# Turning the second half's context and x by small loads and VectorE, the last product token by token, in a new order

## The chip, the cores and the metric

The kernel runs on one core of a Trainium2 chip. The metric is the device time of one execution in microseconds. A core has five engines with instruction queues of their own, each taken in order: TensorE (PE in the profile; its weight loads are the row PEld), VectorE (DVE), ScalarE (ACT), GpSimd (POOL) and SyncE (SP), which here issues every transfer between the large memory (HBM) and the on-chip memory (SBUF). TensorE writes into eight banks of a second on-chip memory, PSUM. All data are 32-bit floats.

## The reference

One cross-attention block with a two-layer network behind it, for 8 sequences of 256 tokens, 512 features, 16 heads of 32. The mask is all ones.

```python
x = layer_norm(hidden_states, ln1_w, ln1_b)
q = (x @ q_w + q_b)                      # 16 heads of 32
k = (encoder_hidden_states @ k_w + k_b)
v = (encoder_hidden_states @ v_w + v_b)
attn = softmax(q k^T / sqrt(32))
out = (attn v) @ cproj_w + cproj_b
hidden = out + hidden_states
y = layer_norm(hidden, ln2_w, ln2_b)
y = gelu(y @ fc_w + fc_b, approximate=True)     # 512 -> 2048
return hidden + (y @ proj_w + proj_b)           # 2048 -> 512
```

## The kernel before

The 2048 tokens are worked through in two halves g = 0, 1 of 1024 tokens (four sequences each). In each half the stages are: context and x come in and are turned so that features lie on partitions; q, k and v are projected; sixteen units of attention follow (four heads of one sequence each); then the output projection (o), the second layer norm (y), the wide layer (fc) and the narrow layer (pd). Stages of the two halves overlap.

**Seven products.** A projection is split into 2 x 2 blocks and worked out as seven block products with sums of blocks around them instead of eight (`quad`, `sums`, `operands`). The products of one quad are called P1 to P7; they collect in three PSUM banks X, Y and W, and VectorE, ScalarE or GpSimd add the banks into four result blocks. The two layers of the network do this twice, seven outer products of seven inner ones (`grown2` for fc, `grown` for pd). All products are issued by one helper, `mm` (the profile's L642); a 32-bit matmul is two instructions in the profile. The sums of weights for the network are made once, by VectorE and GpSimd during the first attention, and stored to HBM (fcd, prd) by SyncE.

**Turning.** `turned` (L713) does it on TensorE: four transposes of 128x128 fill one PSUM bank (L729), and a copy, for x with the layer norm's scale and bias, takes it to SBUF. Context and x of both halves go this way, and y of the first half: eight banks each. `moved` (L734) does it without TensorE, and only y of the second half goes this way: eight stores of normalised tiles to HBM (yd), sixteen loads of 128 KB that bring 32x32 blocks into place in pieces of 128 bytes (yb), eight VectorE transposes of 32x32 blocks over 128x512 (L748), and a pass with scale and bias (L752 on ScalarE, L754 on VectorE).

**The narrow layer's end.** `ending` (L1270 on) runs after four of the seven outer products of pd, when a quarter of the result is complete. The result po lies with features on partitions. For three quarters VectorE turns 32x32 blocks (tr, L1311), adds the residual read back from HBM in 128-byte pieces (rq, out), and SyncE stores it in such pieces (so). The last quarter, features 256 to 511 of the first 512 tokens, is finished by the outer product 4, of the blocks z1t4 and z1i and the weights pl14. In the second half it is turned on TensorE (turn_o, L1289, eight transposes), added to the residual rl (ot), and stored as two tiles (st).

**What sets the order.** PROGRAM lists every step in the order of issue, with the engine behind a colon (V is VectorE, A ScalarE, G GpSimd) where there is a choice; PLACES gives each buffer its slot. Both are tables written out in the kernel. A step's instructions stand in their engine's queue in that order. Buffers share slots, and a name in the profile is that of the slot's first user: `ct` or `q` may hold a weight later on.

## Time and profile before

| what | value |
|---|---|
| median of the runs | 675.18 us (3 runs, 672.50 to 675.52) |
| profiled execution, first to last instruction (span) | 671.4 us |
| median less span | 3.8 us |
| mean granted clock of TensorE | 1.000 of full speed |
| busy: TensorE, VectorE, ScalarE, GpSimd | 662.8, 585.3, 347.3, 345.0 us |
| DMA traffic | 140.97 MB in 174064 packets, 71.9% of 16 engines' span |

The profile is one execution; its own time is the span and what lies around it, and only the span is recorded. A row of the table by windows gives a stretch's start and end, its length, the busy time of TensorE, its weight loads, VectorE, ScalarE and GpSimd with instruction counts in brackets, the granted clock, the busy share of the DMA engines and the rate in GB/s. A group of instructions reads: line, engine, operation, output<-inputs, shapes, count, then busy time and mean nanoseconds, then idle time before them. In the view of one tile, the durations are minimum/median/maximum in ns.

### The profile page before, as it was taken

How to read it: one execution, taken by the hardware profiler on the slowest of the kernel's cores; microseconds unless marked ns; L12 is line 12 of the kernel's file. 1: busy time of each engine (PE TensorE's matmuls, PEld its weight loads, DVE VectorE, ACT ScalarE, POOL GpSimd, SP SyncE). 2: the span in 40 equal slices, each digit the busy share in tenths (PEclk: the TensorE clock that was granted, in tenths of full speed). 3: DMA queues.
4: the chain of work that ended last, by engine and by line, in shares of the span. 5: the costliest groups of instructions: out<-in, count | busy, mean ns of one | idle time of the engine just before them, and what ended most of it. 6: DMA issues, size and time to landing. Idle time of an engine off the chain costs nothing.

```text
span 671.4 us, 11531 instructions
## 1 busy us (share of the span) xinstructions
PE 662.8 (99%) x4001; PEld 497.7 (74%) x4001; DVE 585.3 (87%) x974; ACT 347.3 (52%) x711; POOL 345.0 (51%) x322
## 2 busy tenths in 40 slices
...
GB/s 250 330 291 319 318 285 271 226 290 259 258 186 234 214 136 141 212 273 105 142 111 118 205 158 250 179 254 260 240 206 297 122 240 104 266 80 142 169 186 114
DMA packets 174121, 141.69 MB, mean 211 GB/s; under 512 B 83776, under 2 KB 134512, under 8 KB 174064
## 3 DMA queue, kind: packets, MB, share of 16 engines
q1 hardware_dynamic: 174064, 140.97, 71.9%
...
q14 instruction: 25, 0.20, 0.1%
...
## 4 chain that ended last, share of the span: by engine, by line
PE 86%; DVE 8%; DMA 2%; ACT 2%; SPq 1%; issue 1%; POOL 0%; DVEq 0%; ACTq 0%
PE pd_X L642 14%; PE fc_X L642 14%; PE fc_W L642 7%; PE pd_W L642 7%; PE av L642 7%; PE s L642 4%; PE o_X L642 4%; PE pd_Y L642 4%; PE k_X L642 3%; PE fc_Y L642 3%; PE q_X L642 3%; PE v_X L642 3%; PE v_W L642 2%; DVE mx L1005 2%; PE k_W L642 2%; DMA cq<-in_ctx_dram 2%
## 5 line engine op out<-in xcount | busy, mean ns | idle before, releaser
L622 ACT ACTIVATE pr<-s,cols 128x256 f32<-128x256 f32 x256 | 103.8, 484 | 23.3 <-PE s L642 12.6
L1030 POOL TENSOR_TENSOR pr<-pr,mm 128x512 f32<-128x512 f32 x60 | 76.6, 1307 | 20.0 <-DMA mm<-md 17.0
L1005 DVE TRANSPOSE_TENSOR_REDUCE mx<-pr 128x32 f32<-128x1024 f32 x64 | 77.5, 1223 | 3.8 <-ACT pr L622 3.6
L1033 ACT ACTIVATE pr<-pr 128x1024 f32<-128x1024 f32 x64 | 66.2, 1065 | 7.9 <-DVE pr L1025 5.9
L1210 ACT ACTIVATE h<-h,cols 128x256 f32<-128x256 f32 x128 | 56.2, 501 | 12.0 <-DVE h L633 11.8
L633 DVE TENSOR_TENSOR h<-fc_X,h 128x512 f32<-128x512 f32 x80 | 53.1, 679 | 7.6 <-PE fc_X L642 7.2
L1025 DVE TENSOR_TENSOR pr<-pr,mm 128x1024 f32<-128x1024 f32 x34 | 41.2, 1237 | 0.2 <-DMA mm<-md 0.2
L633 DVE TENSOR_TENSOR h<-fc_W,h 128x512 f32<-128x512 f32 x48 | 32.0, 681 | 6.7 <-PE fc_W L642 6.3
L642 PE MATMUL av<-pr,ones 128*32 128x256 f32 x512 | 34.2, 384 | 0.2
L1012 ACT COPY mx<-mx 32x64 f32<-32x64 f32 x96 | 23.1, 243 | 19.1 <-issue 16.0
L808 ACT ACTIVATE xn_y<-hid,rs_y 128x512 f32<-128x512 f32 x7 | 5.5, 817 | 52.1 <-DVE rs_y L800 52.0
L633 POOL TENSOR_TENSOR h<-h,fl 128x512 f32<-128x512 f32 x12 | 15.6, 1311 | 25.2 <-DVE fl L633 24.9
L642 PEld LDWEIGHTS av<-pr,ones 128*32 128x32 f32 x512 | 14.5, 109 | 18.3 <-issue 4.8
L609 ACT COPY fl<-fc_X 128x512 f32<-128x512 f32 x6 | 3.5, 583 | 40.6 <-PE fc_X L642 38.5
L631 POOL TENSOR_TENSOR z0t<-h,h 128x512 f32<-128x512 f32 x10 | 14.7, 1489 | 11.2 <-issue 10.6
L1013 DVE TENSOR_REDUCE mx<-mx 32x32 f32<-32x256 f32 x32 | 18.3, 575 | 1.2 <-ACT mx L1012 1.0
L633 DVE TENSOR_TENSOR h<-fc_Y,h 128x512 f32<-128x512 f32 x24 | 16.1, 677 | 2.6 <-PE fc_Y L642 2.3
L642 PE MATMUL fc_W<-y1i,fl 128*128 128x256 f32 x72 | 18.1, 380 | 0.0
L633 POOL TENSOR_TENSOR tq<-tq,rq 128x512 f32<-128x512 f32 x8 | 10.1, 1273 | 13.5 <-DVE tq L1311 13.5
L642 PE MATMUL pd_W<-z1i,pl 128*128 128x256 f32 x72 | 16.8, 380 | 0.0
L752 ACT ACTIVATE y<-y,cols 128x512 f32<-128x512 f32 x7 | 5.5, 811 | 21.5 <-DVE y L748 21.5
L642 PE MATMUL fc_X<-y1i,fl 128*128 128x256 f32 x64 | 16.5, 381 | 0.0
...
## 6 DMA issues: line engine op xcount, KB each, us to landing
...
```

Of the source, the lines that this page charges most:

```text
L622: lambda e: nc.scalar.activation(to(), of_(), AF.Identity, bias=bias(), scale=1.0))
L631: nc.gpsimd.tensor_tensor(to()[:, ts(k, 512)], in0()[:, ts(k, 512)], in1()[:, ts(k, 512)], op)
L633: E[e].tensor_tensor(to(), in0(), in1(), op)
L642: nc.tensor.matmul(o(), l(), r(), start=first, stop=True, skip_group_check=True)
L752: nc.scalar.activation(at(r, j, 1, 512), at(r, j, 1, 512), AF.Identity, bias=col(cb_ + c), scale=col(cw_ + c))
L1005: T.op(f"mx{u}_{h}", [("DVE", 1.126)], [(pr[h], None)], [(mx, [h])], lambda e, h=h: nc.vector.tensor_reduce(tile_of(mx)[:, 0:64].rearrange ...
L1012: lambda e, a=a: nc.scalar.copy(tile_of(mx)[0:32, 64 + 64 * a : 128 + 64 * a], tile_of(mx)[32 * a : 32 * a + 32, 64:128]))
L1013: T.op(f"fold{u}", [("DVE", 0.38)], [(mx, [2, 3, 4, 5])], [(mx, [6])], lambda e: nc.vector.tensor_reduce(tile_of(mx)[0:32, 320:352], tile_ ...
L1025: nc.vector.tensor_tensor(p_, p_, m_[:, :, None, :].to_broadcast([P, 2, 2, S]), ALU.subtract)
L1030: E[e].tensor_tensor(p_, p_, at(M, j)[:, None, :].to_broadcast([P, 2, S]), ALU.subtract)
L1033: lambda e, h=h: nc.scalar.activation(tile_of(pr[h]), tile_of(pr[h]), AF.Exp), table="exp")
L1210: lambda e, f=f, b=b, c=c: nc.scalar.activation(at(h[f][b], c), at(h[f][b], c), AF.Gelu_apprx_tanh, bias=col(c_fcb + f * 4 + c), scale=1.0 ...
```

## The change

1. Context and x of the second half go by `moved` instead of `turned`. The context is read in 128-byte pieces straight from its input (cb), with no stores ahead and no scaling pass behind; x is stored after its normalisation (xd), loaded (xb), transposed (xT) and scaled.
2. The inner products of the outer product 4 of the second half's pd swap their operands: the activations are the stationary side, and the weights stream past, so tokens lie on partitions. Each inner product is eight matmuls of 128 columns instead of four of 256. Their sums go straight into the tiles that are stored (ot).
3. What those tiles start from is the quarter as it stands without the product 4, with the residual: VectorE turns it and adds rq, SyncE stores it to a scratch tensor (lo, eight stores) and loads it back (rl, four loads). The transposes on TensorE at the end (turn_o) go. The last stores are three, of one whole tile and two halves.
4. PROGRAM and PLACES are written anew throughout; engines of many steps change, mostly from VectorE to GpSimd. The second batch of warm-up matmuls writes a bank of its own.

The new order at two places. First TensorE's queue at its end, where the last products of pd stand (pd14 is the outer product 4, its banks X, Y, W; ps_o the transposes). Before:

```order
L642 MATMUL pd13_Y_5821<-h1_32_5047,pl13_2_5727 128x256 x4
L642 MATMUL pd14_X_5745<-z1i4_1_5735,pl14_4_5700 128x256 x4
L642 MATMUL pd14_W_5841<-z1i4_3_5803,pl15_3_5591 128x256 x4
L642 MATMUL pd14_X_5745<-z1t4_3_5682,pl14_3_5787 128x256 x4
L642 MATMUL pd14_Y_5857<-z1t4_2_5679,pl13_3_5691 128x256 x4
L1289 MATMUL ps_o11_5865<-ident_64,po1_1_5461 128x128 x2
L1289 MATMUL ps_o01_5869<-ident_64,po1_1_5461 128x128 x2
L642 MATMUL pd14_W_5841<-z1i4_4_5833,pl14_4_5700 128x256 x4
L1289 MATMUL ps_o00_5881<-ident_64,po1_0_5380 128x128 x2
L1289 MATMUL ps_o10_5887<-ident_64,po1_0_5380 128x128 x2
```

And now:

```order
L633 MATMUL pd13_X_5661<-h1_33_5137,pl14_2_5473 128x256 x4
L633 MATMUL pd14_X_5771<-pl15_4_5183,z1t4_0_5676 128x128 x8
L633 MATMUL pd12_W_5714<-z1i2_4_5668,fl107_0_4698 128x256 x4
L633 MATMUL pd14_X_5771<-pl12_3_5501,z1i4_2_5719 128x128 x8
L633 MATMUL pd13_W_5740<-z1i3_4_5749,pl02_4_4365 128x256 x4
L633 MATMUL pd14_X_5771<-pl14_5_5622,z1i4_1_5709 128x128 x8
L633 MATMUL pd14_W_5843<-rl0_5758,z1i4_3_5756 128x128 x8
L633 MATMUL pd14_X_5771<-pl12_1_4994,z1t4_3_5702 128x128 x8
L633 MATMUL pd14_W_5843<-pl13_2_5515,z1i4_4_5814 128x128 x8
L633 MATMUL pd14_Y_5877<-pl14_2_5473,z1t4_2_5578 128x128 x8
```

The eight ps_o transposes are gone; seven groups of eight 128-column matmuls, with z blocks as the second name, take the place of the seven groups of four, and nothing of TensorE's stands behind the last of them.

Second, VectorE's queue where the second half's context comes in, beside the first attention's units (mx and pr are a unit's maxima and scores; c1 the context turned, cb1 as loaded, ps_c1 as transposed by TensorE; the other names are slots that hold q and k sums at that time). Before:

```order
L794 TENSOR_SCALAR rs_x1_0_942<-mv_x1_0_761 128x2
L1025 TENSOR_TENSOR pr000_0_710<-pr000_0_710,mm000_864 128x1024
L1025 TENSOR_TENSOR pr000_1_748<-pr000_1_748,mm000_864 128x1024
L609 COPY c1_10_937<-ps_c1_30_956 128x512
L1005 TENSOR_REDUCE mx022_969<-pr022_1_913 128x2x2x8
L633 TENSOR_TENSOR q0_1_21_731<-q0_1_W_917,q0_1_21_731 128x512
L633 TENSOR_TENSOR v0_0_21_417<-v0_0_W_812,v0_0_21_417 128x512
L1013 TENSOR_REDUCE mx002_879<-mx002_879 32x32
```

And now:

```order
L744 STREAM_TRANSPOSE c1_00_895<-cb1_0_725 128x512
L808 TENSOR_SCALAR q0_1_22_882<-kws1_352,mv_x1_1_776,rs_x1_1_837 128x512
L1011 TENSOR_REDUCE mx020_864<-mx020_864 32x32
L744 STREAM_TRANSPOSE c1_00_895<-cb1_1_620 128x512
L624 TENSOR_TENSOR q0_1_22_882<-q0_1_W_885,q0_1_22_882 128x512
L1003 TENSOR_REDUCE mx002_928<-pr002_0_888 128x2x2x8
L744 STREAM_TRANSPOSE c1_01_846<-cb1_0_725 128x512
L1003 TENSOR_REDUCE mx002_928<-pr002_1_898 128x2x2x8
L1007 STREAM_TRANSPOSE mx002_928<-mx002_928 128x64
L624 TENSOR_TENSOR kw01_359<-v0_0_W_933,kw01_359 128x512
L1003 TENSOR_REDUCE mx022_960<-pr022_1_939 128x2x2x8
L1011 TENSOR_REDUCE mx002_928<-mx002_928 32x32
```

Before, VectorE has one copy of the context here, behind TensorE's transposes, and ScalarE has the other seven; now VectorE has eight transposes that wait for loads, and the maxima of the units 002 and 022 stand between and behind them.

The diff, without the two tables:

```diff
@@ PROGRAM @@
-cq0_00_1 cq0_00_0 rows5 vw00 rows3 kw00 rows6 kw10 turn_c0_00 rows4 turn_c0_10 c0_00:V cq0_01_1 c0_10:V cq0_10_1
...
+cq0_00_0 cq0_00_1 vw00 cq0_01_1 fw0_00_1 cq0_01_0 cq0_11_0 cq0_11_1 vw10 fw0_01_1 turn_c0_00 rows1 turn_c0_10 vw11
@@ -500,6 +490,7 @@
 }
+MOVED = {"c": (1,), "x": (1,), "y": (1,)}
 KINDS = ("pppppppppppppppp", "pppppppppppppppp")
@@ -731,21 +722,28 @@
-    def moved(g, tag, tiles, cw_, cb_):
+    def moved(g, tag, tiles, cw_, cb_, of_=None):
         R = [[Buf(f"{tag}{g}_{J}{L}", "Q", 4) for L in range(2)] for J in range(2)]
-        d = dram(f"{tag}d{g}", [1024, D], 8)
-        for i in range(8):
-            b, f = tiles[i]
-            store(f"{tag}d{g}_{i}", d, [i], [(b, None)], lambda i=i: d.t[ts(i, P), :], f, 0.26)
+        if of_ is None:
+            d = dram(f"{tag}d{g}", [1024, D], 8)
+            src = [(d, None)]
+            for i in range(8):
+                b, f = tiles[i]
+                store(f"{tag}d{g}_{i}", d, [i], [(b, None)], lambda i=i: d.t[ts(i, P), :], f, 0.26)
+        else:
+            src = []
+        whole = (lambda: d.t) if of_ is None else (lambda: of_)
         for c in range(4):
...
                 load(f"{tag}b{g}_{c}{a}", q, [a], lambda q=q, a=a: tile_of(q)[32 * a : 32 * a + 32].rearrange("p (t j) -> p t j", j=32),
-                     lambda a=a, c=c: d.t.rearrange("(t i) (b a j) -> b a i t j", i=32, b=4, a=4)[c, a], 0.33, src=[(d, None)], lead=2.0)
+                     lambda a=a, c=c: whole().rearrange("(t i) (b a j) -> b a i t j", i=32, b=4, a=4)[c, a], 0.33, src=src, lead=2.0)
             for L in range(2):
...
                      lambda e, q=q, r=r, j=j, L=L: nc.vector.transpose(at(r, j, 1, 512), at(q, L, 1, 512)))
+                if cw_ is None:
+                    continue
@@ -1144,7 +1142,7 @@
-    def grown(name, n, place, spare, product_of, cost, wide, before=None, bias={}):
+    def grown(name, n, place, spare, product_of, cost, wide, before=None, bias={}, end=None):
@@ -1153,7 +1151,10 @@
                 dst, add = fused[p]
-                quad(f"{name}{p}", product_of(p), cost, dst, add=add, bias=bias.get(p), n=n, wide=wide)
+                wd = wide
+                if p == 4 and end:
+                    dst, add, wd = end
+                quad(f"{name}{p}", product_of(p), cost, dst, add=add, bias=bias.get(p), n=n, wide=wd)
             else:
@@ -1258,14 +1259,26 @@
                 (lk, lv), (rk, rv) = Lw[q], Ri[q]
+                if g == 1 and p == 4:
+                    return [lk, rk], [
+                        (lambda t=t: bank()[:, ts(t, P)], lambda t=t, c=c: rv()[:, c * 256 + t * P : c * 256 + t * P + P], lambda c=c: lv()[:, ts(c, P)],
+                         first and t == 0 and c == 0)
+                        for t in range(2) for c in range(4)
+                    ]
                 return [lk, rk], [
...
-        rq, tq, view, ot = {}, {}, {}, {}
-        rl = [Buf(f"rl{l}", "P") for l in range(2)] if g == 1 else None
+        rq, tq, view = {}, {}, {}
+        two = lambda t: t.rearrange("p (t n) -> p t n", t=2)
+        if g == 1:
+            rl, ot = [Buf(f"rl{l}", "P", 2) for l in range(2)], [Buf(f"ot{l}", "P", 2) for l in range(2)]
+            part_ = dram("lo", [512, 256], 8)
+
+        def at_end(bufs):
+            return {k: ((bufs[e % 2], [e // 2]), lambda b=bufs[e % 2], i=e // 2: two(tile_of(b))[:, :, ts(i, P)]) for e, k in enumerate(IL)}
@@ -1275,26 +1288,14 @@
             if g == 1 and p == 4:
-                two = lambda t: t.rearrange("p (t n) -> p t n", t=2)
-                for l in range(2):
-                    ot[l] = Buf(f"ot{l}", "P", 2)
-                    load(f"rl{l}", rl[l], None, lambda l=l: two(tile_of(rl[l])),
-                         lambda l=l: h_.t[l * S : (l + 1) * S, ts(I, 256)].rearrange("(t p) n -> p t n", p=P), 0.26, src=[(h_, [l])], lead=3.0)
-                for e in (0, 3, 1, 2):
-                    i, l = divmod(e, 2)
-                    ps = Buf(f"ps_o{i}{l}", "C")
-
-                    def turn(_, ps=ps, l=l, c=2 * I + i):
-                        for t in range(2):
-                            nc.tensor.transpose(tile_of(ps)[:, ts(t, P)], at(po[l], c)[:, ts(t, P)], ident.t)
-                    T.op(f"turn_o{i}{l}", [("PE", 0.225)], [(po[l], [2 * I + i]), (ident, None)], [(ps, None)], turn, mode="full")
-                    plus(f"ot{i}{l}", (ot[l], [i]), (ps, None), (rl[l], None), lambda i=i, l=l: two(tile_of(ot[l]))[:, :, ts(i, P)],
-                         lambda ps=ps: two(tile_of(ps)[:, :256]), lambda i=i, l=l: two(tile_of(rl[l]))[:, :, ts(i, P)], 256)
-                for l in (1, 0):
-                    store(f"st{l}", None, None, [(ot[l], None)], lambda l=l: o_[l * S : (l + 1) * S, ts(I, 256)].rearrange("(t p) n -> p t n", p=P),
-                          lambda l=l: two(tile_of(ot[l])), 0.26)
+                for l, i in ((1, None), (0, 0), (0, 1)):
+                    w = slice(0, 256) if i is None else slice(i * P, i * P + P)
+                    store(f"st{l}{'' if i is None else i}", None, None, [(ot[l], None if i is None else [i])],
+                          lambda l=l, w=w: o_[l * S : (l + 1) * S, 256 + w.start : 256 + w.stop].rearrange("(t p) n -> p t n", p=P),
+                          lambda l=l, w=w: two(tile_of(ot[l]))[:, :, w], 0.26 if i is None else 0.13)
                 return
-            part = (1,) if g == 1 and I else (0, 1)
+            rest = g == 1 and I == 1 and L == 1
+            part = (0, 1)
             last = L == (1 if not I or g else 0)
@@ -1306,17 +1307,28 @@
                              0.165 * len(part), src=[(h_, [2 * x + y for x in part for y in range(2)])], lead=3.0)
-                for l in range(2):
-                    b = 2 * L + l
+                for b in range(4) if rest else (2 * L, 2 * L + 1):
                     T.op(f"tr{g}_{c}{b}", [("DVE", 0.34)], [(po[b], [c])], [(tq[c], [b])], lambda e, b=b, c=c: nc.vector.transpose(at(tq[c], b), at(po[b], c)))
-                plus(f"out{g}_{c}{L}", (tq[c], [2 * L, 2 * L + 1]), (tq[c], [2 * L, 2 * L + 1]), (rq[c], None), lambda c=c: at(tq[c], L, 1, 512),
-                     lambda c=c: at(tq[c], L, 1, 512), lambda c=c: at(rq[c], L, 1, 512), 512, pool_too=True)
-                if last:
+                for h in (0, 1) if rest else (L,):
+                    plus(f"out{g}_{c}{h}", (tq[c], [2 * h, 2 * h + 1]), (tq[c], [2 * h, 2 * h + 1]), (rq[c], None), lambda c=c, h=h: at(tq[c], h, 1, 512),
+                         lambda c=c, h=h: at(tq[c], h, 1, 512), lambda c=c, h=h: at(rq[c], h, 1, 512), 512, pool_too=True)
+                if rest:
+                    half = lambda t, a, h: t[32 * a : 32 * a + 32, 512 * h : 512 * h + 512].rearrange("p (t j) -> p t j", j=32)
+                    piece = lambda m, a, r0, c0: m[r0 : r0 + 512, c0 + 32 * a : c0 + 32 * a + 32].rearrange("(t i) j -> i t j", i=32)
+                    for a in range(4):
+                        store(f"lo{i}{a}", part_, [4 * i + a], [(tq[c], [0, 1])], lambda i=i, a=a: piece(part_.t, a, 0, i * P), lambda c=c, a=a: half(tile_of(tq[c]), a, 0), 0.17)
+                    for a in range(4):
+                        store(f"so{g}_{c}{a}", None, None, [(tq[c], [2, 3])], lambda c=c, a=a: piece(o_, a, 512, c * P), lambda c=c, a=a: half(tile_of(tq[c]), a, 1), 0.17)
+                    for l in range(2):
+                        load(f"rl{l}{i}", rl[l], [i], lambda l=l, i=i: two(tile_of(rl[l]))[:, :, ts(i, P)],
+                             lambda l=l, i=i: part_.t[l * S : (l + 1) * S, ts(i, P)].rearrange("(t p) n -> p t n", p=P), 0.13, src=[(part_, [4 * i + a for a in range(4)])], lead=2.0)
+                elif last:
                     for a in range(4):
...
         grown(f"pd{g}", 256, place, spare, product_of, 1.727, lambda t: t[:, :256], ending,
-              {p: {k: (lambda c=c_pb + 2 * I + e // 2: col(c)) for e, k in enumerate(IL)} for p, I in ((2, 0), (3, 0), (7, 1))})
+              {p: {k: (lambda c=c_pb + 2 * I + e // 2: col(c)) for e, k in enumerate(IL)} for p, I in ((2, 0), (3, 0), (7, 1))},
+              (at_end(ot), at_end(rl), lambda t: two(t[:, :256])) if g == 1 else None)
@@ -1328,15 +1340,16 @@
         if g == 0:
-            T.op("small", [("PE", 0.1)], [], [], lambda e: small(WARM2))
-        ct = token_quarters(g, "c", ef) if g == 0 else token_tiles(g, "c", ef)
+            again = Buf("again", "W")
+            T.op("small", [("PE", 0.1)], [], [(again, None)], lambda e: small(WARM2, tile_of(again)))
+        ct = token_quarters(g, "c", ef) if g == 0 else token_tiles(g, "c", ef) if g not in MOVED["c"] else None
         if g == 0:
             biases()
-        C = turned(g, "c", ct if g == 0 else [(b, lambda b=b: tile_of(b)) for b in ct], plain)
+        C = turned(g, "c", ct if g == 0 else [(b, lambda b=b: tile_of(b)) for b in ct], plain) if g not in MOVED["c"] else moved(g, "c", None, None, None, ef[g * 1024 : g * 1024 + 1024, :])
         T.stream(f"x{g}")
...
         xn = layer_norm(g, "x", [(b, None, lambda b=b: tile_of(b)) for b in xt])
-        X = turned(g, "x", xn, scaled(c_ln1w, c_ln1b))
+        X = turned(g, "x", xn, scaled(c_ln1w, c_ln1b)) if g not in MOVED["x"] else moved(g, "x", xn, c_ln1w, c_ln1b)
         T.stream(f"k{g}")
@@ -1392,7 +1405,7 @@
         yn = layer_norm(g, "y", srcs)
-        Y = moved(g, "y", yn, c_ln2w, c_ln2b) if g in (1,) else turned(g, "y", yn, scaled(c_ln2w, c_ln2b))
+        Y = moved(g, "y", yn, c_ln2w, c_ln2b) if g in MOVED["y"] else turned(g, "y", yn, scaled(c_ln2w, c_ln2b))
         for b in range(4):
...
```

676 lines of the change are left out of this document (333 added, 343 removed).

## The prediction

> **What bounds the kernel now.** I read the page's busy table first, then what TensorE waited for.
>
> ```profile
> span 671.4 us, 11531 instructions
> ...
> PE 662.8 (99%) x4001; PEld 497.7 (74%) x4001; DVE 585.3 (87%) x974; ACT 347.3 (52%) x711; POOL 345.0 (51%) x322
> ...
> q1 hardware_dynamic: 174064, 140.97, 71.9%
> ```
>
> ```profile
> engine line waited for: us in total, times, longest us
> PE ps_y L729 <- DVE rs_y L794: 1.2, 1, 1.2
> PE first L654 <- DVE warm L649: 1.0, 1, 1.0
> PE v_X L642 <- DVE kw L609: 0.5, 1, 0.5
> PE fc_W L642 <- DVE h L633: 0.4, 1, 0.4
> ...
> PE fc_Y L642 <- DVE y L767: 0.2, 1, 0.2
> ```
>
> TensorE is busy 99% of the span and its longest wait is 1.2 us. A busy matmul engine can still run slowly, so I looked in the chain of waits, in order of time, at the pace of whole stretches (start, length, what):
>
> ```profile
> 56.47 1.75 PE ps_x L729 x16
> ...
> 93.98 2.18 PE ps_c L729 x20
> ...
> 457.37 5.18 PE pd_W L642 x24
> ```
>
> A 256-column matmul instruction takes 5.18/24 = 0.216 us, a 128-column transpose 1.75/16 = 0.109 us: time goes as columns, with nothing between. So TensorE bounds the kernel from end to end, and what leaves it leaves the time, as long as the others keep feeding it. How near they are to not doing so, by stage:
>
> ```profile
> core 0: us, PE busy (x) PEld busy (x) DVE busy (x) ACT busy (x) POOL busy (x), PEclk, DMA share, GB/s
> 20.00:60.00 40.00, 39.72 (x143) 23.98 (x142) 37.92 (x74) 16.04 (x25) 16.31 (x20) 1.00 0.93 314
> 60.00:100.00 40.00, 40.00 (x226) 23.01 (x225) 36.80 (x61) 27.18 (x65) 13.39 (x16) 1.00 0.91 306
> 100.00:180.00 80.00, 79.44 (x603) 48.33 (x605) 75.70 (x125) 66.89 (x138) 55.06 (x55) 1.00 0.84 260
> 180.00:260.00 80.00, 79.76 (x668) 48.33 (x664) 76.29 (x128) 74.68 (x165) 63.51 (x53) 1.00 0.61 193
> ```
>
> From 20 to 180 us VectorE idles 9.6 us of 160, and the DMA engines have 40 x 0.07 + 40 x 0.09 + 80 x 0.16 = 19.2 us free. The new work falls into just this stretch.
>
> **Context and x leave TensorE.** Each had eight turns of four 128-column transposes: 64 x 0.109 = 6.98 us of TensorE gone, with the waits between them. Eight PSUM copies go for the context, seven of them ScalarE's; x keeps its scaling as a pass of its own, a copy from PSUM against a pass over SBUF, about even. VectorE gets 16 transposes of 128x512:
>
> ```profile
> L596 SPq DMA_DIRECT2D yb<-yd x16: 302/560/1617, 475.0 to 493.0; - x16
> L748 DVE STREAM_TRANSPOSE y<-yb x8: 664/683/702, 489.3 to 503.9; 128x512 f32<-128x512 f32 x8
> ```
>
> That is 16 x 0.683 = 10.9 us. The new order pays for it: counted in the two programs, VectorE has 111 instead of 134 sums of 128x1024 with both inputs in SBUF, and GpSimd 232 instead of 181 of 128x512.
>
> ```profile
> L1030 POOL TENSOR_TENSOR pr<-pr,mm 128x512 f32<-128x512 f32 x60 | 76.6, 1307 | 20.0 <-DMA mm<-md 17.0
> ...
> L1025 DVE TENSOR_TENSOR pr<-pr,mm 128x1024 f32<-128x1024 f32 x34 | 41.2, 1237 | 0.2 <-DMA mm<-md 0.2
> ```
>
> VectorE: 10.9 - 23 x 1.237 = 17.6 us less; GpSimd: 51 x 1.307 = 66.7 us more of its 326 idle. On their own neither is the bound, so I cost them at nothing; the cover is the idle time just named, and the rivals price its loss.
>
> **The loads.** Context: 8 loads of 256 KB become 16 of 128 KB in 128-byte pieces. x: 8 stores of 256 KB and 16 such loads are added to its loads. The 256 KB transfer costs, at 314 GB/s (20 to 60 us), 0.83 us of all engines. For the small pieces, the second y gives the price, five of its loads in a row on SyncE's queue:
>
> ```profile
> 474.98 4.12 SPq L596 DMA_DIRECT2D yb<-yd  x5
> ```
>
> 0.82 us for each 128 KB. Context adds 16 x 0.82 - 8 x 0.83 = 6.5 us, x 16 x 0.82 + 8 x 0.83 = 19.8 us: 26.3 us against 19.2 free, 7.1 too many. The bounds are nothing (fill-in traffic, the weight sums' stores, steps aside; some loads of x now go out in the first 20 us) and 7.1 us. In the fullest stretch before, 0.93, TensorE lost only 0.28 us of 40, so I take 2.0, nearer to nothing. What waits behind a late load is told by VectorE's rows: two transposes of the context stand ahead of the softmax maxima (TENSOR_REDUCE mx) of the units 002 and 022, and VectorE takes its queue in order; each such wait stops scores, then TensorE. On SyncE's queue an xd store that waits for its normalised tile holds the broadcasts (mm) of the next units. Of x the chain is longer by a store and a load; the order answers by normalising its first tiles some 50 us of TensorE work sooner. If that cover fails, the second half's q products wait.
>
> **The last product by tokens.** Its seven products are now 112 instructions of 128 columns instead of 56 of 256, each with its own weight load. By the transposes' pace they take 112 x 0.109 = 12.2 us, against 56 x 0.216 = 12.1: 0.1 us more. The weight loads, min/median/max ns:
>
> ```profile
> L729 PEld LDWEIGHTS ps_x<-ident,xn_x x20: 139/141/146, 47.6 to 177.1; 128*128 128x128 f32 x20
> ```
>
> ```profile
> L642 PEld LDWEIGHTS v_X<-vw,c x32: 186/190/190, 7.7 to 141.2; 128*128 128x128 f32 x32
> ```
>
> A transpose's load of 141 ns hides under 109 ns streams; a product's takes 190. Nothing in this trace pairs a product's 128-column load with a 128-column stream, so the bounds are 0.109 and 0.190 us each, 0 to 9.1 us in all. The nearest row is the warm-up, 64-column loads under 64-column streams:
>
> ```profile
> 5.89 1.85 PE L654 MATMUL first<-warm 128*64 128x64 f32 x28
> 7.67 1.56 PE L642 MATMUL v_X<-vw,c 128*128 128x256 f32 x6
> ```
>
> 28 in 7.67 - 5.89 = 1.78 us, 0.064 each for half the columns: near the stream's pace, so I take 0.1 us. The Trainium skill, "TensorE: Matmul & The Clock Gate", section "Back-to-back issue gap", says that a stream with a weight load for each matmul is paced by both, about 81 ns where the stream alone is 56 at 128 columns. By that rule, as an estimate, 25 ns x 112 = 2.8 us would be added; the transposes' 109 ns speak against it here.
>
> **The end.** Start, length, engine, operation:
>
> ```profile
> 664.44 0.60 PE L1289 MATMUL ps_o<-ident,po 128*128 128x128 f32 x4
> ...
> 664.88 1.89 PE L642 MATMUL pd_W<-z1i,pl 128*128 128x256 f32 x8
> ...
> 666.61 0.38 PE L1289 MATMUL ps_o<-ident,po 128*128 128x128 f32 x2
> 666.81 0.42 DVE L633 TENSOR_TENSOR po<-pd_W,po 128x256 f32<-128x256 f32 x1 [0.97 <-PE pd_W L642]
> 667.15 0.41 DVE L633 TENSOR_TENSOR ot<-ps_o,pl 128x256 f32<-128x256 f32 x1
> 667.29 0.20 PEld L1289 LDWEIGHTS ps_o<-ident,po 128*128 128x128 f32 x2 [0.54 <-DVE po L633]
> ...
> 667.76 0.43 DVE L633 TENSOR_TENSOR ot<-ps_o,pl 128x256 f32<-128x256 f32 x1 [0.20 <-PE ps_o L1289]
> 668.22 0.39 SPq L602 DMA_DIRECT2D out_dram<-ot  x1
> ```
>
> Four transposes stand ahead of the last product: 664.88 - 664.44 = 0.44 us gone. From that product's last slot, 666.61, to the end at 671.4 pass 4.79 us: sum, transpose, sum, store. Without the transpose: 0.20 to the sum, 0.42 for it, 0.03 to the issue, 671.4 - 668.22 = 3.18 for the store, 3.83 in all, 0.96 less. The residual's way by TensorE is replaced by four VectorE transposes, eight small stores and four loads, done before the last outer product ends; they cost nothing while the stores ahead of the last one drain in time.
>
> **The sum.** 671.4 - 6.98 - 0.44 - 0.96 + 0.1 + 2.0 = 665.1 us of span. The median of the runs shown, 675.18, lies 3.8 above the span; so 668.9 us. A measurement can tell about 0.5% (3.4 us) of this kernel from no change.
>
> **Rivals.** *More than the sum.* The new order is free to close the old waits too. TensorE's nine listed waits, five of them shown, come to 4.3 us, 3.3 without the warm-up's; with the loads hidden (no 2.0) the time is 675.2 - 8.3 - 3.3 = 663.6. For: they lie on VectorE, which gets lighter. Against: every new order makes waits of its own.
>
> *The loads give it back.* All 7.1 us reach TensorE: 675.2 - 8.3 + 7.1 = 674.0, no difference. For: the shares of 0.84 to 0.93. Against: no wait of TensorE for a DMA there before.
>
> *The loads turn it round (slower).* The same queue, but 128-byte pieces among full traffic cost more than 0.82. The overload is 7.1 + 32 x (c - 0.82); it passes 8.3 + 3.4 = 11.7, slower by 0.5%, at c = 0.96 us. One issue of the y loads took 1.617 us on the queue. At c = 1.1 it is 16.1 us, 683 in all. Against: the y loads kept 0.82 while the queues were full.
>
> *VectorE and GpSimd shut each other out.* GpSimd's sums are 1274 ns or far longer:
>
> ```profile
> L631 POOL TENSOR_TENSOR c1t<-c,c1t x4: 1274/1716/2266, 101.2 to 119.1; 128x512 f32<-128x512 f32 x4
> ...
> L633 DVE TENSOR_TENSOR c1t<-c,c x1: 1204/1204/1204, 99.9 to 99.9; 128x1024 f32<-128x1024 f32 x1
> ```
>
> 2266 - 1274 = 0.99 us is most of one such VectorE sum. Up to the first output projection GpSimd has 145 of these instead of 120; if each of the 25 costs VectorE 0.99 us, that is 24.7 us, against 9.6 idle from 20 to 180 and 3.7 from 180 to 260: 11.4 us over, 675.2 - 8.3 + 11.4 = 678.3, no difference. The Trainium skill, "SBUF — State Buffer", section "Who interferes with whom", says that a VectorE instruction with two SBUF inputs and a GpSimd one that reads SBUF cannot run at once. By that rule, the trace agrees (2266 against 1274 ns). Against this rival: VectorE's own such sums get fewer by 23.
>
> *The token-major product is paced by its weight loads*, at 0.190 us each: 9.1 us in place of 0.1, so 668.9 + 9.0 = 677.9, no difference; below 2.9 us of it, still faster (671.8). For: the 190 ns. Against: the warm-up's pace.
>
> **How the numbers follow.** The forecast 0.57; more than the sum 0.14; the loads give it back 0.12; the shut-out 0.07; weight-load pace 0.04; slower by late loads 0.06. Faster takes the first two and half of the weight-load case: 0.73; no change 0.21; slower 0.06. The range goes from 662.5 (old waits closed, a little more at the end) to 677.0 (give-back, and most of the shut-out); it leaves out the late loads and little below.
>
> **What would show it.** Right: a span near 665; no ps_c or ps_x of the second half; seven token-major groups of 1.74 us at the end; about 3.8 us after the last product; no VectorE wait for the context's small loads over 2 us. Wrong: token-major groups near 3 us; TensorE waiting between 60 and 180 us behind VectorE, with the DMA share at 1 there; GpSimd's 128x512 sums well over 1.31 us on the mean.

## The result, and the profile after

| | before | after |
|---|---|---|
| median (14 runs each) | 672.88 us | 678.92 us |
| lowest and highest | 672.10, 675.52 | 674.87, 683.51 |
| profiled span | 671.4 us | 677.6 us |

The ratio is 1.0082 (95%: 1.0062 to 1.0101): slower by 0.8%, where 668.9 us against 675.18, 0.9% less, was forecast. An execution's time lies about 1.8 us above its own span (1.75 to 1.91 in after's fourteen), not 3.8: the 3.8 set the median of three executions against the span of another. That made the forecast of the time too high, so its miss of 10.0 us hides 2.5 of the 12.5 us by which the span was missed (677.6 against 665.1). The page of after, in the lines that the prediction began with (busy time, share, instructions; then the DMA queue):

```profile
span 677.6 us, 11590 instructions
...
PE 660.0 (97%) x3985; PEld 495.9 (73%) x3985; DVE 579.9 (86%) x956; ACT 343.6 (51%) x703; POOL 445.6 (66%) x380
...
q1 hardware_dynamic: 216480, 146.21, 76.7%
```

TensorE is busy 2.8 us less in a span that is 6.2 us longer. What it waited for, the longest first:

```profile
engine line waited for: us in total, times, longest us
PE k_X L633 <- DVE kws L624: 2.8, 1, 2.8
PE av L633 <- ACT pr L1031: 1.5, 4, 0.5
PE pd_X L633 <- DVE z0i L624: 1.3, 2, 1.0
PE fc_W L633 <- DVE e L624: 1.1, 1, 1.1
```

There are 17 such rows and 13.0 us, where before had nine and 4.3. One wait is long; the rest are scattered over the kernel, and behind them stand all four other parties. By stage (columns as in the table of before):

```profile
core 0: us, PE busy (x) PEld busy (x) DVE busy (x) ACT busy (x) POOL busy (x), PEclk, DMA share, GB/s
20.00:60.00 40.00, 37.18 (x137) 23.60 (x136) 33.15 (x68) 13.81 (x22) 24.00 (x27) 0.96 1.02 358
60.00:100.00 40.00, 39.88 (x170) 21.46 (x169) 36.99 (x60) 26.23 (x60) 23.23 (x23) 1.00 0.99 269
100.00:180.00 80.00, 78.74 (x626) 46.91 (x625) 73.91 (x129) 64.32 (x134) 70.25 (x62) 1.00 1.00 278
180.00:260.00 80.00, 77.59 (x575) 46.90 (x573) 75.97 (x117) 74.32 (x163) 70.87 (x54) 1.00 0.76 241
```

The DMA engines are full to 180 us, and from 100 us on GpSimd works 141 of 160 us, where it worked 119. The groups that grew or came (count, busy us, mean ns, idle before):

```profile
L1028 POOL TENSOR_TENSOR pr<-pr,mm 128x512 f32<-128x512 f32 x78 | 108.0, 1413 | 13.6 <-DMA mm<-md 7.0 <-PE fc_X L633 5.9 <-issue 0.5
L1023 DVE TENSOR_TENSOR pr<-pr,mm 128x1024 f32<-128x1024 f32 x25 | 32.1, 1294 | 0.8 <-DMA mm<-md 0.8
...
L744 DVE STREAM_TRANSPOSE y<-yb 128x512 f32<-128x512 f32 x8 | 5.5, 697 | 6.2 <-DMA yb<-yd 6.2
L744 DVE STREAM_TRANSPOSE c<-cb 128x512 f32<-128x512 f32 x8 | 5.3, 684 | 0.0
L744 DVE STREAM_TRANSPOSE x<-xb 128x512 f32<-128x512 f32 x8 | 5.2, 672 | 0.0
```

The transposes of context and x cost what was forecast (10.5 us, 10.9 forecast) and wait for no load. But the same softmax subtraction is 8% dearer on GpSimd than in before (1413 against 1307 ns) and 5% on VectorE (1294 against 1237).

The end went nearly as forecast. The timeline (start, length):

```profile
668.26 1.95 PE L633 MATMUL pd_X<-pl,z1t 128*128 128x128 f32 x16
...
670.05 1.95 PE L633 MATMUL pd_W<-pl,z1i 128*128 128x128 f32 x16
...
671.83 1.95 PE L633 MATMUL pd_Y<-pl,z1t 128*128 128x128 f32 x16
...
673.82 0.42 DVE L624 TENSOR_TENSOR pl<-pd_Y,pl 128x256 f32<-128x256 f32 x1 [1.36 <-PE pd_Y L633]
674.27 0.37 SPq L593 DMA_DIRECT2D out_dram<-pl  x1
```

A token-major group starts 1.79 us after the one ahead of it (1.74 forecast). The prediction counted the end from the last product's last slot; that is 671.83 + 1.79 = 673.62 here, and from there to the span's end pass 3.96 us (4.79 before, 3.83 forecast).

**Where the time went.** For each run of like instructions on TensorE I took the time to the next run's start, less its count by the pace of undisturbed stretches (0.109, 0.216, 0.430 us for 128, 256, 512 columns; 0.058 for warm-up; attention 1.80 us for 32 av and 1.08 for 16 scores). What is left is TensorE's lost time, waits and slow clock alike, in us by stage; records missing from a trace count in it, so some tenths mean nothing.

| kernel | 0-40 | 40-120 | 120-260 | 260-480 | 480-600 | 600- | all |
|---|---|---|---|---|---|---|---|
| before | 3.5 | 2.1 | 6.2 | 7.5 | 1.6 | 0.2 | 21.1 |
| after | 10.3 | 2.2 | 11.3 | 5.2 | 5.4 | 1.1 | 35.4 |
| before_48_out | 3.1 | 5.0 | 11.2 | 8.9 | 1.6 | 0.2 | 30.0 |
| before_48_out_less | 3.7 | 3.8 | 8.1 | 6.1 | 1.6 | 0.2 | 23.4 |
| before_72_added | 3.2 | 1.7 | 4.8 | 8.5 | 1.6 | 0.2 | 20.0 |
| after_72_added | 7.0 | 3.6 | 7.3 | 5.9 | 6.1 | 1.1 | 31.1 |
| after_all_relieved | 7.2 | 2.0 | 8.9 | 6.0 | 5.5 | 1.1 | 30.7 |

So TensorE's own work fell by 7.7 us (72 transposes fewer, 7.85, and 0.1 more for the token-major groups), the end by another 0.4 (0.83, less 0.44 for the four transposes that stood in it), and its lost time rose by 14.3: together the 6.2 us of span. The loss came at three places: the first 40 us, the first attention (120 to 260), and the second half's wide layer (480 to 600). Of the 10.3 us in the first 40, some 3 belong to this execution. The trace records its full clock from 10.36 us on, before's from 5.44 (28 warm-up matmuls took from 6.71 to 10.15 us here, from 5.89 to 7.67 in before), and the clock was halved again behind the wait of 2.8 us. The seven other profiles with after's unchanged start lose 6.6 to 7.3 there.

### The profile page after: what moved, and what is told of

The parts are those of the page before. It is cut to its first block, busy times and chain, and to the rows that moved or that the text cites. A ratio compares the mean times of both kernels' runs of the same rounds, so it can differ in the third digit from the quotient of the medians.

```text
span 677.6 us, 11590 instructions
## 1 busy us (share of the span) xinstructions
PE 660.0 (97%) x3985; PEld 495.9 (73%) x3985; DVE 579.9 (86%) x956; ACT 343.6 (51%) x703; POOL 445.6 (66%) x380
## 4 chain that ended last, share of the span: by engine, by line
PE 68%; DVE 11%; DMA 8%; ACT 5%; POOL 3%; issue 2%; SPq 2%; DVEq 0%; POOLq 0%; ACTq 0%
PE fc_X L633 11%; PE pd_X L633 11%; PE av L633 6%; PE pd_W L633 6%; PE fc_W L633 5%; PE q_X L633 3%; PE s L633 3%; PE fc_Y L633 3%; PE v_X L633 3%; PE o_X L633 3%; PE pd_Y L633 2%; ACT pr L613 2%; DMA fw<-in_L_xattn_fc_w_dram 2%; PE k_X L633 2%; SPq L587 2%
## 5 line engine op out<-in xcount | busy, mean ns | idle before, releaser
L1028 POOL TENSOR_TENSOR pr<-pr,mm 128x512 f32<-128x512 f32 x78 | 108.0, 1413 | 13.6 <-DMA mm<-md 7.0
L624 DVE TENSOR_TENSOR h<-fc_X,h 128x512 f32<-128x512 f32 x80 | 53.6, 680 | 14.1 <-PE fc_X L633 12.9
L1023 DVE TENSOR_TENSOR pr<-pr,mm 128x1024 f32<-128x1024 f32 x25 | 32.1, 1294 | 0.8 <-DMA mm<-md 0.8
L622 POOL TENSOR_TENSOR z1i<-z1t,z1i 128x512 f32<-128x512 f32 x8 | 11.8, 1494 | 17.8 <-DVE z1i L624 17.8
L624 POOL TENSOR_TENSOR tq<-tq,rq 128x512 f32<-128x512 f32 x9 | 11.9, 1330 | 12.8 <-DVE h L624 6.0
L622 POOL TENSOR_TENSOR z0t<-h,z0t 128x512 f32<-128x512 f32 x6 | 10.4, 1750 | 14.5 <-DVE z0t L624 14.5
L750 ACT ACTIVATE y<-y,cols 128x512 f32<-128x512 f32 x5 | 4.0, 813 | 30.9 <-DVE y L744 30.9
L633 PE MATMUL fc_X<-y1i,fl 128*128 128x256 f32 x72 | 18.4, 380 | 0.5 <-DVE h L624 0.5
L633 PE MATMUL pd_W<-z0i,pl 128*128 128x256 f32 x80 | 18.8, 380 | 0.0
L633 PE MATMUL pd_X<-z0i,pl 128*128 128x256 f32 x72 | 16.9, 380 | 1.0 <-DVE z0i L624 1.0
L624 POOL TENSOR_TENSOR po<-po,e 128x256 f32<-128x256 f32 x7 | 6.9, 1001 | 15.2 <-DVE e L624 11.1
```

The lines of the kernel that those rows point to most:

```text
L622: nc.gpsimd.tensor_tensor(to()[:, ts(k, 512)], in0()[:, ts(k, 512)], in1()[:, ts(k, 512)], op)
L624: E[e].tensor_tensor(to(), in0(), in1(), op)
L633: nc.tensor.matmul(o(), l(), r(), start=first, stop=True, skip_group_check=True)
L1023: nc.vector.tensor_tensor(p_, p_, m_[:, :, None, :].to_broadcast([P, 2, 2, S]), ALU.subtract)
L1028: E[e].tensor_tensor(p_, p_, at(M, j)[:, None, :].to_broadcast([P, 2, S]), ALU.subtract)
```

## The experiments

Ratios are to before's runs on the same chip, with 95% intervals; after itself was not timed again beside each of them, so a comparison with it takes its 1.0082 as it stands. The theories, in the order in which they were formed: **A**, the new order loses in its first 40 us, and that stays to the end. **B**, the 128-byte loads fill the DMA engines. **C**, VectorE and GpSimd shut each other out. **D**, VectorE paces the first attention as much as TensorE does, so TensorE's time is not worth its time. **E**, TensorE bounds the kernel and after has many small waits. **F**, several engines are at their limit together. **G**, each mended place keeps what it gains.

**The first 40 us (A).** VectorE's and TensorE's timelines of after at the place:

```profile
25.51 1.23 DVE L624 TENSOR_TENSOR fw0s<-fw,fw 128x1024 f32<-128x1024 f32 x1 [3.92 <-DMA fw<-in_L_xattn_fc_w_dram]
26.65 0.68 DVE L624 TENSOR_TENSOR kws<-kws,kw 128x512 f32<-128x512 f32 x1
```

```profile
27.48 3.62 PE L633 MATMUL k_X<-c0t,kws 128*128 128x512 f32 x4 [2.82 <-DVE kws L624]
```

A sum of fc weights, needed far later, stands in VectorE's queue ahead of kws and waits 3.92 us for its load; TensorE waits 2.82 for kws. kws_first turns the two round:

```diff
-fw1_11_0 fw0s1:V k0_1_t1:A xt0_1 qw00 v0_1_P6 xt0_6 kws2:V xt0_4
+fw1_11_0 k0_1_t1:A xt0_1 qw00 v0_1_P6 xt0_6 kws2:V fw0s1:V xt0_4
```

> One step of VectorE moved, nothing else: the k weights' sum kws2 goes ahead of the fc weights' sum fw0s1, for which VectorE waited 3.9 us on a load. Theory A (the new order loses, first of all in its first 40 us): TensorE's 2.8 us wait for kws and the 3.41 us at half clock behind it (1.7 us lost) go, unless the context's late load then stops TensorE in their place; 675 to 677 us against 679 of the changed kernel. Theory B (the 128-byte loads of context and x fill the queue and cost it): no change, 679. Theory C (VectorE and GpSimd shut each other out): no change, 679.

Measured: 1.0106 (1.0084 to 1.0127). The wait is gone, and another has come (where the tables differ, so do the line numbers):

```profile
23.53 1.88 PE L622 MATMUL k_X<-c0t,kws 128*128 128x512 f32 x4
29.09 1.09 PE L709 MATMUL ps_c<-ident,cq 128*128 128x128 f32 x8 [3.68 <-DMA cq<-in_ctx_dram]
```

The products start 4 us sooner and then wait 3.68 us for a piece of the context whose load stands behind fc weights in SyncE's queue. So fw_later also moves the first eight fc loads and the sums that need them behind the loads of context, k and v:

```diff
-cq0_00_0 cq0_00_1 vw00 cq0_01_1 fw0_00_1 cq0_01_0 cq0_11_0 cq0_11_1 vw10 fw0_01_1 turn_c0_00
+cq0_00_1 cq0_00_0 vw00 cq0_01_1 cq0_01_0 cq0_11_0 cq0_11_1 vw10 turn_c0_00
...
+vw01 cq0_10_1 vws2:V k0_1_P7 cq0_10_0 kw01 fw0_00_1 fw0_01_1 fw0i2_1:G fw0_10_0 fw0_11_1 fw0_00_0
...
+fw0i1_1:V fw0i1_2:V fw0i1_4:G fw0s1:V fcd0_5_False fw0s2:V fw0s3:V
```

> The first eight fc weight loads and their sums on VectorE go behind the loads of the context, of k's and of v's weights, and the first two loads of the context swap places as they stood before. Theory A: the start comes back to what it lost before the change, 6.7 us less, so 672 to 673 us. Theory B: the same bytes are moved later, into the stretch that the small loads fill already: no gain, 679 or more. Theory C: 679.

Measured: 1.0118 (1.0094 to 1.0142). Up to 30 us TensorE has lost 3.2 us by the measure of the table, as much as in before, where the seven profiles with after's unchanged start have lost 6.3 to 7.1. The lead does not last: up to 38 us it is 6.1 against 6.5 to 7.1, up to 60 us 8.6 against 6.5 to 7.8. (After's own profile, 4 us behind at 38 us, is a poor standard: some 3 of these are its late and halved clock.) Four places of fw_later's TensorE queue:

```profile
34.52 1.99 PE L622 MATMUL v_X<-vws,c 128*128 128x256 f32 x8 [2.57 <-POOL vws L613]
...
54.75 0.33 PE L709 MATMUL ps_x<-ident,xn_x 128*128 128x128 f32 x1 [1.88 <-DVE xt L613]
...
55.84 0.70 PE L622 MATMUL k_W<-c0t,vw 128*128 128x512 f32 x1 [0.43 <-DVE vw L613]
...
125.93 1.07 PE L622 MATMUL av<-pr,ones 128*32 128x256 f32 x16 [2.63 <-ACT pr L1020]
```

A lead is worth nothing here, since what feeds TensorE does not come sooner too. start_mended makes fewer moves (two context loads and two weight loads ahead of fc loads, kws first).

```diff
+rows4 fw0_00_1 cq0_10_1
...
+rows5 fw0_01_1 cq0_10_0
...
+rows2 fw0_10_0 fw0_11_1 vw01 fw0_00_0 kw01
...
+kws2:V fw0s1:V
```

> The changed kernel with the start mended more gently than in the run with the fc weight loads later: the context's last two loads and the v and k weights' last loads go ahead of six of the fc weight loads, the context's first loads stand as before, the sum kws2 goes ahead of fw0s1, and one fc sum each of VectorE and GpSimd goes a few places back. TensorE's two waits at 24 to 30 us (kws, 1.0 to 2.8 us; the context's late load, 0.3 to 1.1 us) should go, with some of the 3 us that the first 10 us cost. Theory D (VectorE takes back what the start gains, in the first attention): under 1.5 us, 677 to 679. Theory G (waits are a matter of place, each mended one stays mended): 3 us or more, 675 to 676.

Measured: 1.0121 (1.0084 to 1.0158), no better than after. But TensorE still waits for kws,

```profile
24.30 3.62 PE L622 MATMUL k_X<-c0t,kws 128*128 128x512 f32 x4 [2.32 <-DVE kws L613]
```

and loses 7.4 us in the first 40, no less than the seven. So three moved starts left the time where it was, but only fw_later gained anything, and only up to 34 us. A is neither shown nor refuted: after and all its variants lose 6.1 us or more in the first 40, before and its variants 3.1 to 3.7, and no run carried a mended start past that point.

**The small loads (B).** wide_loads brings the same bytes of the second half's context and x in contiguous pieces of 4096 bytes:

```diff
-  lambda a=a, c=c: whole().rearrange("(t i) (b a j) -> b a i t j", i=32, b=4, a=4)[c, a]
+  lambda a=a, c=c: whole().rearrange("(b a i r) j -> b a i r j", b=4, a=4, i=32)[c, a].rearrange("i r j -> i (r j)")
```

> The changed kernel, but the second half's context and x are loaded in pieces of 4096 bytes from contiguous rows instead of 128 bytes: same bytes, same number of transfers, features in the wrong places. Theory A: within 1 us of 679. Theory B: the 26.3 us of extra DMA time fall to about 20 x 0.83 = 13 or so, and the time by 4 us or more, to 675 or less. Theory C: 679.

Measured: 1.0074 (1.0046 to 1.0103). The DMA engines are relieved (0.82 and 0.89 where after has 0.99 and 1.00), and the time is not:

```profile
60.00:100.00 40.00, 39.88 (x179) 20.81 (x181) 36.98 (x61) 25.15 (x58) 23.48 (x24) 1.00 0.82 276
100.00:180.00 80.00, 77.39 (x608) 46.38 (x609) 72.72 (x126) 63.60 (x133) 65.87 (x60) 1.00 0.89 274
```

The time is 0.5 us below after's (2.3 either way), where B asked for 4 or more (the 13 us it names are 16 x 0.83, not 20). B fell, and with it the rivals of the prediction that put the loss on full DMA engines. From 20 to 60 us they stay full in this run too (1.04), so on that stretch it says nothing.

**What TensorE's time is worth in before (D against E).** before_48_out leaves out 48 of the 64 transposes in question, 48 x 0.109 = 5.2 us, and nothing else of before's order; the copies read the first tile's tokens four times.

```diff
-for i, (_, _, f) in enumerate(tt):
+for i, (_, _, f) in enumerate(tt[:1] if g == 1 else tt):
```

> The kernel before, with 48 of the 64 transposes of the second half's context and x left out: each bank gets only the tokens of its first tile, and the copy reads them four times over. No load, no order, no other engine changes. If TensorE's time is the time (the first step of the prediction): 48 x 0.109 = 5.2 us less, 667.7 us against 672.9. If the other engines are so near that a shorter TensorE only waits more: 2 us or less of it is seen.

Measured: 1.0024 (1.0008 to 1.0040). Taking 5.2 us from the engine that is busy 99% made the kernel 1.6 us slower (0.5 to 2.7). The profile is of the slowest of its twelve executions (676.92, with a median of 675.52), so its losses are larger than the usual ones. They show from 180 to 260 us

```profile
180.00:260.00 80.00, 77.42 (x620) 46.66 (x612) 78.33 (x120) 72.68 (x162) 73.15 (x52) 1.00 0.59 189
```

and in one group of GpSimd's sums:

```profile
L633 POOL TENSOR_TENSOR pw1i<-pw1s,pw1i 128x256 f32<-128x256 f32 x3 | 9.8, 3261 | 0.1
```

The same group in before:

```profile
L633 POOL TENSOR_TENSOR pw1i<-pw1s,pw1i 128x256 f32<-128x256 f32 x3 | 2.2, 731 | 0.1
```

VectorE is busy 78.3 of 80 us (76.3 in before) and GpSimd 73.2 (63.5), for much the same work: two of these three sums took 4.67 and 4.40 us. In before's row of this stage VectorE idles 3.7 us; I read this as 5.2 us sooner being more than the stage had to give; no run isolates it.

before_less and before_48_out_less then narrow VectorE's own softmax subtractions of the first attention to a quarter, without and with the transposes left out:

```diff
-nc.vector.tensor_tensor(p_, p_, m_[:, :, None, :].to_broadcast([P, 2, 2, S]), ALU.subtract)
+w = 64 if u[0] == "0" else S
+nc.vector.tensor_tensor(p_[:, :, :, :w], p_[:, :, :, :w], m_[:, :, None, :w].to_broadcast([P, 2, 2, w]), ALU.subtract)
```

> The kernel before; in the first half's attention the subtractions of the maxima that VectorE does take 64 of every 256 columns, so some 23 of its 128x1024 sums shrink from 1.24 to about 0.4 us (19 us of VectorE); the exponential's scale is 0.01, at the same cost. Theory D (up to about 170 us VectorE's queue, slowed by GpSimd, paces the first attention as much as TensorE does, and the order only fills TensorE's time around it): a little is gained, the waits of 100 to 280 us, 2 to 4 us, 669 to 671. Theory E (TensorE is the bound, and the losses of the runs so far are waits that a new order scatters): less than 1.5 us, 672 to 673.

> Both cuts together: the kernel before with 48 of 64 transposes left out, and VectorE's subtractions of the first attention narrowed to 64 of 256 columns (exponential's scale 0.01). Theory D: now the transposes are worth their time, 5.2 us below the kernel with the narrowed subtractions alone, 664 to 666 us. Theory E: 673 to 675, as with the transposes out alone.

Measured: 0.9996 (0.9980 to 1.0012) and 0.9958 (0.9943 to 0.9974). Relieving VectorE alone is worth nothing; relieving TensorE alone is worth nothing; both together give 2.6 us against VectorE relieved alone (1.5 either way), half of the 5.2. The stage in before_48_out_less, and then the group:

```profile
180.00:260.00 80.00, 78.72 (x659) 47.62 (x657) 70.86 (x131) 74.09 (x163) 63.72 (x53) 1.00 0.63 194
```

```profile
L633 POOL TENSOR_TENSOR pw1i<-pw1s,pw1i 128x256 f32<-128x256 f32 x3 | 2.2, 725 | 0.1
```

The converse: before_72_added and after_72_added put four idle transposes into the bank ahead of 18 products of the second half's k, v and q, 72 x 0.109 = 7.85 us of TensorE.

```diff
+idle = 4 if name[:2] in ("k1", "v1", "q1") and "_P" in name and items[0][3] else 0
...
+for _ in range(idle):
+    nc.tensor.transpose(items[0][0]()[:, :P], ident.t, ident.t)
```

> The kernel before with TensorE work added instead of taken away: 72 idle transposes of the identity, four into the bank ahead of each of the 18 products of the second half's k, v and q that begin a bank, so 72 x 0.109 = 7.85 us between 100 and 230 us; nobody reads them, and no other engine or order changes. If TensorE's time is the time there: 7.8 us more, 1.0117 of the kernel before. If the other engines set the pace as much (theory D): a part of it is hidden in the waits, 4 to 6 us.

> The same 72 idle transposes in the changed kernel, ahead of the same 18 products: TensorE gets back what the change took from it. If TensorE's time is the time there: 7.8 us more, 1.020 of the kernel before. If it is not (theory D: there the transposes' time was already turned into waits): 3 us or less more, at most 1.0127 of the kernel before.

Measured: 1.0070 (1.0053 to 1.0087) and 1.0086 (1.0066 to 1.0106). In before, 7.85 us added cost 4.7. In after they cost 0.0004, 0.3 us (by the two intervals, 1.9 either way). This is the run that decides: where the transposes left, at most about 2 of 7.85 us of TensorE's time count in after. E fell. The stage from 100 to 180 us in before_72_added,

```profile
100.00:180.00 80.00, 80.00 (x617) 50.44 (x616) 73.37 (x120) 63.00 (x130) 50.89 (x50) 1.00 0.78 243
```

has no idle TensorE at all, and in after_72_added

```profile
100.00:180.00 80.00, 79.81 (x663) 49.71 (x664) 71.37 (x125) 62.94 (x132) 66.95 (x60) 1.00 1.00 276
```

it is nearly as full: the added transposes fill what were gaps (lost time 120 to 260: 7.3 us, 11.3 in after). This profile is of the slowest of six executions, 3.5 us longer than after's, so that 0.3 us rests on the times and not on it.

**Which engine paces after (C, D, F).** after_less narrows VectorE's subtractions as above, after_less_gpsimd GpSimd's, after_relieved both and with the wide loads, after_all_relieved ScalarE's exponentials of the first attention as well.

```diff
-E[e].tensor_tensor(p_, p_, at(M, j)[:, None, :].to_broadcast([P, 2, S]), ALU.subtract)
+E[e].tensor_tensor(p_[:, :, :w], p_[:, :, :w], at(M, j)[:, None, :w].to_broadcast([P, 2, w]), ALU.subtract)
```

> The changed kernel; VectorE's 17 subtractions of the first attention narrowed to 64 of 256 columns (exponential's scale 0.01): some 14 us of VectorE less. Theory D: the excess of 100 to 280 us goes and the start's loss is no longer given back twice: 5 us or more, 674 or less. Theory E: 677 to 679.

> The changed kernel; GpSimd's subtractions of the first attention narrowed to 64 of 256 columns instead of VectorE's (exponential's scale 0.01): VectorE has as many instructions as before, but GpSimd stands in its way less. If the loss is that the two shut each other out (theory C as the way by which D happens): VectorE's 128x1024 sums fall from 1294 towards 1237 ns on the mean, and the time by 4 us or more, to 675 or less. If VectorE is slow for its own work alone: 678 to 679.

> The changed kernel with the three reliefs at once: the subtractions of the first attention narrowed to 64 of 256 columns on VectorE and on GpSimd (exponential's scale 0.01), and the second half's context and x loaded in pieces of 4096 bytes, their features in the wrong places. Each alone gave nothing. Theory F (several engines and the queue are each at their limit in the first 260 us, so that one relieved leaves the next): now 4 us or more come out, 675 or less. Theory G (the new order's waits are a matter of latency and of where steps stand, not of how much any engine has to do): 677 to 680 again.

> As the changed kernel with the three reliefs, and ScalarE's exponentials of the first attention narrowed to 64 of 256 columns too (32 of them, some 0.7 us each), so that in 100 to 260 us every engine but TensorE has clearly less to do. If the sum of the engines' work sets the time (theory D or F with ScalarE as the one left): TensorE's excess of 11 to 12 us between 120 and 260 us falls under 7, and the time to 674 or less. If it is place and latency (theory G): 677 to 679.

Measured, in this order: 1.0081 (1.0048 to 1.0115), 1.0107 (1.0058 to 1.0156), 1.0061 (1.0037 to 1.0086), 1.0037 (1.0011 to 1.0064). Neither engine's relief alone did anything that shows, so D for after fell. C was tested in part only: GpSimd's relief should have made VectorE's sums faster, and they were not (1294 ns on the mean in after):

```profile
L1023 DVE TENSOR_TENSOR pr<-pr,mm 128x1024 f32<-128x1024 f32 x25 | 32.4, 1308 | 2.9 <-DMA mm<-md 2.9
```

From 60 to 260 us 17 of VectorE's 30 sums of 128x1024 or 30 of GpSimd's 81 of 128x512 were narrowed, and none in the rest of the kernel. With all four relieved, 0.0045 or 3.0 us came back (2.2 either way), half of the loss. Its second stage:

```profile
180.00:260.00 80.00, 78.84 (x649) 48.55 (x651) 71.49 (x131) 68.41 (x164) 57.95 (x53) 1.00 0.72 226
```

TensorE gains 1.25 us of busy time there on after's 77.59, with 4.5, 5.9 and 12.9 us less work on the other three. That is for F, but it is half of the loss only.

fw_later_less and both_mended_less join VectorE's relief to the mended start (and, in the second, to the mended second half below), so as to see whether a lead is kept.

> The fc weight loads moved behind those of the context, k and v, as before, and VectorE's subtractions of the first attention narrowed as before (64 of 256 columns, exponential's scale 0.01). With the loads alone TensorE stood 4.2 us ahead at 38 us and had given it all back by 137 us, at waits for VectorE. If VectorE is what it ran into (theory D): the lead is kept, 674 to 676. Theory G: given back at other waits, 679 to 681.

> Both mended, and VectorE's subtractions of the first attention narrowed to 64 of 256 columns (exponential's scale 0.01). Theory D: only now the start's gain is kept through the first attention: 3 us or more below the kernel with both mended, 673 to 674. Theory G: the same as without it, within 1 us.

Measured: 1.0082 (1.0050 to 1.0114) and 1.0109 (1.0075 to 1.0143), no better than after_less. Only fw_later_less has a lead, 2.8 us lost up to 30 us against the 6.3 to 7.1 of the unchanged start, and it is gone by 38 us (7.4), at a wait for GpSimd with half clock behind it:

```profile
34.88 2.82 PE L622 MATMUL v_X<-vws,c 128*128 128x256 f32 x8 [3.21 <-POOL vws L613]
```

So neither run brought a lead as far as the first attention, and D's word that it is kept there stays untested.

**The second half's wide layer (G).** VectorE's queue in after there, and what TensorE waits for:

```profile
486.69 0.71 DVE L744 STREAM_TRANSPOSE y<-yb 128x512 f32<-128x512 f32 x1 [3.58 <-DMA yb<-yd]
487.33 1.18 DVE L624 TENSOR_TENSOR z0i<-z0t,z0i 128x1024 f32<-128x1024 f32 x1
```

```profile
488.56 1.78 PE L633 MATMUL pd_X<-z0i,pl 128*128 128x256 f32 x7 [1.04 <-DVE z0i L624]
```

A transpose that is not yet needed waits 3.58 us for its load, and the sum that TensorE waits for stands behind it. second_half_mended puts this transpose and three more such steps a few places back; both_mended has that and start_mended's moves.

```diff
-fl117_0 yT1_10
...
-z0i4_2:V y1_10:A
...
+pd03_c22 yT1_10 y1_10:A
...
-gelu1_023 z1i1_3:V
...
+fc104_c11 z1i1_3:V
...
-rq1_11 z1i1_2:V
...
+fc104_P7 z1i1_2:V
```

> The changed kernel with four steps of VectorE moved back a little in its queue from 480 us on, each ahead of a sum that TensorE waited for: the first transpose of the second y (VectorE waited 3.58 us for its load, with a sum for pd behind it), one sum with the residual (1.74 us for its load, sums of fc's banks behind it) and two 128x1024 sums of the narrow layer. TensorE's waits there were 1.04, 1.10, 0.70 and 0.50 us. Theory G: here the other engines have time, what is mended stays mended, 2 to 3 us less, 676 to 677. Theory F: TensorE is not what sets the time here either: under 1 us.

> The mended start and the four steps of the second half together. Theory D: the second half's 1.3 us and little more, 676.5 to 678. Theory G: the sum of both, 673.5 to 675, about the kernel before.

Measured: 1.0048 (1.0023 to 1.0073) and 1.0090 (1.0062 to 1.0119). The lost time from 480 to 600 us fell from 5.4 to 3.7 and to 2.2 us. In both_mended_less, which has the same moves, it is 4.8: the mended waits are gone, and waits for loads of weights (one of 1.4 us) have come. For the first the time is 2.3 us under after's (2.1 either way); for the second it is not. So the mended place may have been kept, and these runs do not settle it.

**The change without its order.** before_context_moved keeps before's order and takes only the context by small loads and VectorE: 32 transposes leave TensorE (3.5 us), and eight VectorE transposes stand where the copies stood.

```diff
-pw0i1_3:G turn_c1_20
...
-q0_1_c22 c1_20:A
+q0_1_c22 cT1_20
...
-mc002_1 turn_c1_30
...
-q0_1_P4 c1_30:V
+q0_1_P4 cT1_30
```

> The kernel before with one part of the change: only the second half's context goes by small loads (16 and, for a quarter of it, 8 of half size instead of 4, since no slot of full size is free) and eight transposes on VectorE, each where the copy from PSUM stood; 32 transposes leave TensorE, ScalarE loses seven copies, VectorE one; nothing else moves. The prediction's working: 32 x 0.109 = 3.5 us less, 669.5 to 671. Theory D (TensorE's time converts only where VectorE is light; VectorE gains 4.8 us of work at 95% busy): no gain or a loss, 673 to 677.

Measured: 1.0192 (1.0162 to 1.0222), with a span of 683.9. Waits of TensorE, and then one of VectorE, whose transpose into the context waits for its load (pw0i and q are the slots' names):

```profile
PE k_X L512 <- DVE c L645: 3.5, 1, 3.5
PE s L512 <- ACT pr L492: 3.1, 1, 3.1
PE q_W L512 <- DVE vws L503: 1.9, 1, 1.9
```

```profile
DVE pw0i L503 <- DMA q<-in_ctx_dram: 6.2, 1, 6.2
```

The lost time from 40 to 120 us is 16.7 us, 2.1 in before. Some 6.8 of it are half clock: the trace records a granted clock of 0.50 for 10.24 us from 88.8 us on and for 3.41 us from 109.3 on, behind the waits of 3.1 and 3.5 us. So the rival of late loads in VectorE's queue is real, with its place and a price, 12.5 us of span over before. After starts these loads at 57.6 us, this run at 70.0, and in after VectorE waits for none of them. Whether before's order with earlier loads would have kept the gain, no run shows.

## Why the prediction was wrong

- **Failed: "TensorE bounds the kernel from end to end, and what leaves it leaves the time".** The term -6.98 rests on it. TensorE's own work did fall by that much, and lost time took its place. Before stands at a knee: 5.2 us less of TensorE gave +1.6, 7.85 more cost only 4.7, and 5.2 less with VectorE relieved gave -2.6. The busy share of 99% showed that TensorE hardly ever waited, not that the others could have fed it faster. The prediction's own row said so: 3.7 us of VectorE's 80 were idle from 180 to 260 us.
- **Mis-sized: the 2.0 us for covered work.** TensorE's lost time rose by 14.3 us, which is 12.3 of the 12.5 us by which the span was missed. I had cost the new order, and 66.7 us more of GpSimd work, at nothing because each engine had idle time of its own. GpSimd's busy time rose by 100.6 us, and VectorE's fell by 5.4, not by 17.6. In good part that is because the sums became longer on both: taken over the whole kernel, VectorE's of 128x1024 with both inputs in SBUF from 1269 to 1362 ns on the mean, GpSimd's of 128x512 from 1354 to 1453. How this adds up to 14.3 us of lost time, the runs do not show.
- **The loads.** Right that they fill the DMA engines (share 0.99 and 1.00), and that VectorE waits for none of the context's; wrong that this would be what costs. wide_loads took the overload away from 60 us on and gave nothing that shows.
- **Right: the last product and the end**, 1.79 us a group and 3.96 us at the end, where 1.74 and 3.83 were forecast. The Trainium skill, "TensorE: Matmul & The Clock Gate", section "Back-to-back issue gap", would have had the groups paced by their weight loads too; the estimate of 2.8 us drawn from it is not borne out by 0.05 x 7 = 0.35 us here.
- **The rivals.** Shut-out came nearest in its number (678.3), by luck: it charged VectorE with 24.7 us in the first part, and from 60 to 260 us VectorE's 30 such sums became 1.8 us longer in all (1285 against 1225 ns each). Its signs are there all the same, over the whole kernel, and no run took them away: in after and all its variants VectorE's sums of 128x1024 take 1338 to 1379 ns. How much of the loss it is stays open. The weight-load pace is near by luck too (677.9): a group would have taken 16 x 0.190 = 3.04 us, not 1.79. Late loads did not occur in after.
- **The base**: 3.8 us between span and time, where each execution shows about 1.8. The mistake is in the forecast's favour, as the result says.

**What stays open.** Which resource holds after's pace. It isn't TensorE's own work between 100 and 230 us (after_72_added), and it isn't VectorE, GpSimd or the DMA engines alone as far as the runs relieved them. All of them with ScalarE relieved give about half back. The some 3 us lost in the first 40, the longer sums of VectorE and GpSimd, and the loops through several engines and shared buffers in the first attention are candidates that no run here isolates; and profiles of one kernel vary by some 3 us, which hides smaller things.
